# A graph network's edge sweep: node columns in the count windows in place of part columns and a placing matrix

## Chip, cores and metric

One core of a Trainium2 chip runs the whole kernel. The metric is the device time of one execution in microseconds; the kernel before took 1702.9 us (median of three runs, 1701.83 to 1708.91). The engines are called PE (matrix products; PEld is its weight load), VectorE (DVE in the rows), ScalarE (ACT), GpSimd (POOL) and SyncE (SP).

## What is computed

One graph convolution over 6,250 nodes of 256 features and 200,000 edges sorted by destination, a residual product, a top-2 mixture of 64 experts, a batch norm and a layer norm. What matters here is the sum over edges:

```python
deg_out = jnp.clip(jax.ops.segment_sum(ones, src, num_segments=n), 1.0)
deg_in = jnp.clip(jax.ops.segment_sum(ones, dst, num_segments=n), 1.0)
h = feats * jax.lax.rsqrt(deg_out)[:, None]
m = jax.ops.segment_sum(h[src], dst, num_segments=n) * jax.lax.rsqrt(deg_in)[:, None]
gc = m @ W_gc + b_gc
x = gc + (feats @ W_res + b_res)
```

The destinations are drawn as 6250 times a squared uniform number, so low node numbers have many edges and high ones few. The kernel moves the product with `W_gc` ahead of the sum.

## The kernel before

The stages follow each other: out-degrees and projections (to 176 us of the profile), the sweep over the edges, routing, experts, norms. The change lies in the sweep, in `gnn_moe_kernel` and in `_plan`, which lays the sweep out when the program is built.

The sorted edges form 1,563 groups of 128 (one edge per partition). The plan cuts them in two. The first groups, whose destinations lie close together, are *dense*: they are counted. The rest are *gathered*.

A dense chunk is a window of 128 columns. It has n parts, each of k groups whose destinations span at most w nodes; `DENSE` lists (first group, k, w, n). For each group PE multiplies (`count`, L665) a one-hot of the source's row within its tile (`lo`, made by `lo_of` on VectorE, eight groups a call, L250) with a one-hot of source tile and destination within the part (`hotk`, made by `hot_of`, L652), into a PSUM bank `pc` of 128 x 50 x w numbers: how many edges go from a source to a node. `hot_of` makes as many groups in one call as fit in `LANES // w`, made even; `KB` buffers hold the calls, four banks hold `pc`. After a part's last group ScalarE copies the bank into the chunk's `counts` (L676) at a column that it reads from `places` (a register load per eight parts, L673). Columns are nodes plus the part's number: each part has columns of its own, and a node that two parts share stands twice. Then `multiply` takes the 50 source tiles (L681, L682: the count tile is the weight, the rows `hrow`, in two pieces that add up to full precision, are the moving side) and sums them in one bank. ScalarE copies the sums (L692), and `spread`, at tile 9 of the next chunk, multiplies them by a placing matrix `to` (L698; made on VectorE at L685 from `spos`, which a count of parts per column, `held`, corrects), which adds the columns of one node, and adds the rows that the chunk in front has already summed for the same nodes (the carry-over, `overd`, L700). `sums_done` copies the result and SyncE writes it to `z_dram`.

The gathered groups go in windows of 128 nodes from the last node down: GpSimd fetches 128 rows of 2 KB by index (`fetch`, L580) into a ring of eight tiles, VectorE makes a one-hot for four groups a call (L846), PE adds them up (L585, L586), and a carry-over product (L867) joins the windows.

The order of the sweep is written out by hand: a list of steps with planned costs. Chunk c + 1 is counted while chunk c is multiplied, its parts spread over the tiles 1 to 42:

```python
for j in range(n):
    todo.setdefault(1 + j * 42 // n, []).extend(range(g0 + j * k, g0 + j * k + k))
```

and gathers are put in evenly over the planned time, from 76 us on (`LEAD`):

```python
while n < len(rows) and now > LEAD + n * every:
    gather(n)
    n += 1
```

`x_step` adds, in some of the chunks, the choice of experts for two tiles of finished nodes: ten VectorE calls (`x_make`, `x_top`), two calls on ScalarE, four transposes and eight small products. What it has not done by the end of the sweep is left to the routing stage.

Of the kernel before, what the change touches and what calls it, by code (L numbers as in the profile page):

```python
# [75 lines left out]
def _plan():  # L76
# [16 lines left out]
    def fits(g, k, w, n):  # L93
        return span(g + (n - 1) * k, k) <= w and spread(g, (n - 1) * k) + n + w <= WIN

    def cost(k, w, n):
        return max(12.6 + n * k * (0.021 + w * 0.0208), 5.0 + n * (0.2 + w * 0.03))

    dense, g, pe = [], 0, 0.0
    while 16.0 + 1.03 * (pe + (NGU - g) * 0.265) < (NGU - g) * 1.42:  # L100
        best = None
        for w in range(2, 11):
            for k in range(1, 12):
# [7 lines left out]
                c = cost(k, w, n) - 0.265 * n * k  # L111
# [23 lines left out]
LANES = 36  # L135
# [11 lines left out]
def gnn_moe_kernel(ctx, tc, x_in, src, dst, bases, nexts, firsts, parts, lasts, W_gc, b_gc, W_res, b_res, Wg, bg, w1, b1, w2, b2,  # L147
# [23 lines left out]
    def f32(ap):  # L171
        return ap.bitcast(F32)
# [43 lines left out]
    with tc.tile_pool(name="edges", bufs=1) as ep, ExitStack() as later:  # L216
# [7 lines left out]
        spos = ep.tile([128, ND], F32, name="spos")  # L224
# [38 lines left out]
        with tc.tile_pool(name="late", bufs=1) as lp, tc.tile_pool(name="both", bufs=2) as bp, \  # L263
# [6 lines left out]
            ones_b = dp.tile([128, 1], BF16, name="ones_b")  # L270
            V.memset(ones_b, 1.0)
# [45 lines left out]
            for c, (g0, k, w, n) in enumerate(DENSE):  # L317
                S.activation(rows_w[:, 2, c:c + 1], ones[:, c:c + 1], AF.Copy, scale=float(n - 1 + w))
            S.activation(rows_w[:, 1, :], rows_w[:, 0, :], AF.Copy, scale=-1.0, bias=float(WIN - 1))
            at_or_past = {}  # L320
# [3 lines left out]
            pidx1 = dp.tile([128, 1], F32, name="pidx1")  # L324
            G.tensor_scalar(pidx1, pidx, 1.0 - 64.0, None, op0=ALU.add)
            half_b = dp.tile([128, 1], BF16, name="half_b")
            G.memset(half_b, 0.5)
            npos = dp.tile([128, ND], F32, name="npos")
# [46 lines left out]
            def windows():  # L375
# [9 lines left out]
                G.tensor_tensor(spos, first[:, :ND], neg[:, :ND], ALU.add)  # L385
                V.scalar_tensor_tensor(pos, part[:, 0, :], pidx, first[:, :ND], op0=ALU.add, op1=ALU.subtract)
                G.tensor_scalar(npos, pos, -1.0, 0.5, op0=ALU.mult, op1=ALU.add)
                G.tensor_tensor(okc, okc, first[:, :ND], ALU.subtract)
                G.tensor_tensor(okc, okc, rows_w[:, 2, :], ALU.add)
                G.tensor_tensor(part[:, 1, :], part[:, 1, :], part[:, 0, :], ALU.subtract)  # L390

            def off_parts():
                V.tensor_tensor(away[:, 0, :], part[:, 1, :], rows_w[:, 0, :], ALU.is_gt)
                V.tensor_scalar(away[:, 1, :], part[:, 1, :], 0.0, None, op0=ALU.is_lt)
                V.tensor_add(away[:, 0, :], away[:, 0, :], away[:, 1, :])

            def off_windows():
                V.tensor_scalar(away[:, 1, :], okc, float(WIN), None, op0=ALU.is_gt)
# [7 lines left out]
            def placed():  # L406
# [7 lines left out]
                V.scalar_tensor_tensor(spos, spos, pidx1, held, op0=ALU.add, op1=ALU.subtract)  # L414


            CG, FIRST_IND = 32, 9
            degp = ps_deg.tile([128, 2 * NT], F32, name="degp")
            held = ps_deg.tile([128, ND], F32, name="held")
# [37 lines left out]
            assert FIRST_IND + ND < NGR // CG  # L457
# [9 lines left out]
            for i in range(NGR // CG):  # L467
# [22 lines left out]
                if i >= FIRST_IND:  # L490
                    c = i - FIRST_IND
                    if c < ND:
                        at_or_past[c] = dp.tile([128, 128], BF16, name="ind", bufs=2)
                        S.activation(at_or_past[c], iota_f, AF.Sign, bias=npos[:, c:c + 1])
                    if 1 <= c <= ND:
                        T.matmul(held[:, c - 1:c], at_or_past[c - 1], half_b, start=True, stop=True)
                    if c == ND:
                        placed()
# [47 lines left out]
            V.tensor_scalar(okc, okc, pidx, None, op0=ALU.is_gt)  # L546
# [13 lines left out]
        with tc.tile_pool(name="xs", bufs=1) as xs, tc.tile_pool(name="hotg", bufs=2) as hg, \  # L560
# [32 lines left out]
            def sums_done(pg, c):  # L593

                res = rsp.tile([WIN, D + 2], F32, name="resd" if c < ND else "resg")
                S.copy(res, pg)
# [3 lines left out]
                return res  # L600

            ends_met = {}

# [30 lines left out]
            KB = 2  # L634
            hots, los, live = {}, {}, {}

            def lo_of(q):

                if q * PAIRS < GD:
# [966 lines left out]
```

## Time and profile before

| | us |
|---|---|
| median of three runs | 1702.9 |
| the profiled execution | 1725.73 |
| its span, first to last instruction | 1723.7 |
| PE busy | 1485.0 (86%) |
| VectorE busy | 925.1 (54%) |
| ScalarE busy | 710.7 (41%) |
| GpSimd busy | 877.0 (51%) |

The time of the profiled execution is 2 us longer than its span; it is 1.3% above the median of the runs. A view gives start and length in us of an instruction (or of several like ones, x2), its engine, line, operation and tiles, and in brackets how long the engine stood idle before it and what ended that. PE's ends are modelled: starts are what tells its pace. The granted clock of PE is a share of its upper level, 2.4 GHz. The view by stretch gives for each stretch its length and the busy times of PE, PEld, DVE, ACT and POOL, each with its count of instructions, then the granted clock, the busy share of the DMA engines and what they moved in GB/s.

### The profile page before, as it was taken

Reading aid. Unit: us, or ns where it says so; the run is one execution under the profiler, and the core shown is the slowest. Engines: PE = TensorE matmul, PEld = TensorE weight load, DVE = VectorE, ACT = ScalarE, POOL = GpSimd, SP = SyncE. Lnnn points to the kernel's source line nnn. Section 1 sums busy time; section 2 is a strip of 40 time slices with the busy share of each in tenths; the row PEclk is TensorE's granted clock in tenths of the full one; section 3 lists DMA queues with packets and bytes.
Section 4 is the critical chain, followed back from the end, with each engine's and each line's share of the span. In section 5 each row is a group of like instructions: output and inputs, shape, how many; then the busy total and the mean of one; then the engine's idle time right before and its main releaser. Section 6 shows DMA issues by size and latency. Waiting matters only on the chain. (4 is left out here: it accounts for less than half of the span.)

```text
span 1723.7 us, 31285 instructions
## 1 busy us (share of the span) xinstructions
PE 1485.0 (86%) x10475; PEld 1246.4 (72%) x10475; DVE 925.1 (54%) x1790; ACT 710.7 (41%) x1740; POOL 877.0 (51%) x918
## 2 busy tenths in 40 slices
PE   6999587889999999999999986579999999999730
PEld 3555476778888889898988885368878877777620
DVE  9999865655564555554544545922222222221796
ACT  3443643434565555455554442222222222222248
POOL 6000137776776767667777752046655656554000
PEclk9999679999999999999999997689999999999875
DMA  6899766667767777777767764648868887775924
GB/s 183 255 275 264 221 192 173 184 187 212 202 199 195 203 205 205 207 203 209 204 197 202 207 181 116 165 145 259 244 206 253 268 251 241 205 244 168 240 78 131
DMA packets 217941, 352.50 MB, mean 205 GB/s; under 512 B 24214, under 2 KB 148886, under 8 KB 217770
## 3 DMA queue, kind: packets, MB, share of 16 engines
q1 hardware_dynamic: 158422, 180.22, 35.7%
q0 software_dynamic: 52448, 163.08, 33.3%
q10 hardware_dynamic: 6900, 7.10, 1.5%
q8 instruction: 86, 1.41, 0.3%
q14 instruction: 85, 0.70, 0.1%
HBM read 269.43 MB, written 74.47 MB: 200 GB/s over the span
## 5 line engine op out<-in xcount | busy, mean ns | idle before, releaser
L580 POOL DMA_INDIRECT r<-h_dram,srcg x502 | 558.3, 1112 | 285.9 <-issue 131.6
L681 PE MATMUL sm<-hrow,counts 125*128 125x258 f32 x1650 | 539.9, 344 | 7.6 <-ACT counts L676 7.4
L676 ACT CAST counts<-pc 128x300 f32 (+7 forms) x840 | 376.4, 448 | 323.4 <-PE pc L665 161.1
L682 PE MATMUL sm<-hrow,counts 125*128 125x256 f32 x1650 | 445.7, 286 | 1.6 <-issue 1.6
L681 PEld LDWEIGHTS sm<-hrow,counts 125*128 125x128 f32 x1650 | 328.0, 199 | 33.7 <-issue 18.8
L665 PE MATMUL pc<-hotk,lo 128*128 128x300 bf16 (+7 forms) x1061 | 298.6, 318 | 61.8 <-issue 35.1
L652 DVE TENSOR_TENSOR hotk<-key,iota_h 128x1800 bf16<-128x1800 f16 (+5 forms) x209 | 201.2, 963 | 248.6 <-PE pc L665 117.0
L682 PEld LDWEIGHTS sm<-hrow,counts 125*128 125x128 f32 x1650 | 322.6, 195 | 2.4 <-issue 1.2
L1360 ACT ACTIVATE hT<-ph,b1c 128x128 f32<-128x128 f32 (+8 forms) x256 | 108.3, 437 | 350.9 <-PE ph L1358 202.5
L1370 PE MATMUL py<-w2s,hT 128*128 128x256 f32 (+3 forms) x992 | 241.9, 386 | 7.8 <-ACT hT L1360 5.6
L1358 PE MATMUL ph<-xgT,w1s 128*128 128x128 f32 (+8 forms) x1024 | 210.7, 349 | 3.5 <-ACT hT L1360 2.2
L1370 PEld LDWEIGHTS py<-w2s,hT 128*128 128x128 f32 (+3 forms) x992 | 166.3, 176 | 50.0 <-issue 7.8
L1358 PEld LDWEIGHTS ph<-xgT,w1s 128*128 128x128 f32 x1024 | 170.4, 192 | 37.2 <-issue 15.3
L1324 POOL DMA_INDIRECT y_dram<-ys,dest x124 | 120.0, 968 | 139.8 <-DVE ys L1373 69.0
L1324 POOL DMA_INDIRECT xg<-x_dram,ids x124 | 120.1, 969 | 104.7 <-DVE ids L1275 65.4
L585 PE MATMUL pg<-r,hot 128*128 128x258 f32 x502 | 167.0, 333 | 6.2 <-DVE hot L846 2.5
L665 PEld LDWEIGHTS <-lo 128*128 128x128 bf16 x1061 | 95.6, 105 | 85.4 <-issue 23.6
L1373 DVE TENSOR_TENSOR ys<-py,b2s 128x256 f32<-128x256 f32 (+3 forms) x124 | 51.4, 420 | 175.8 <-PE py L1370 112.2
L586 PE MATMUL pg<-r,hot 128*128 128x256 f32 x502 | 142.7, 284 | 0.0
L1348 DVE COPY xgT<-pte 128x256 f32<-128x256 f32 (+7 forms) x64 | 38.5, 601 | 171.5 <-PE pte L1346 72.9
L846 DVE TENSOR_TENSOR hot<-keyg,iota_f 128x512 fp32r<-128x512 f16 (+3 forms) x135 | 87.7, 651 | 49.9 <-PE pc L665 20.6
L250 DVE TENSOR_TENSOR lo<-lo_b,iota 128x1024 bf16<-128x1024 bf16 x133 | 91.1, 686 | 43.2 <-PE pc L665 31.9
(325 smaller groups left out, 1755.4 us busy)
## 6 DMA issues: line engine op xcount, KB each, us to landing
w1s<-in_L_gnn_w_dram SPq DMA_DIRECT2D x64, 512.0 KB
w2s<-in_L_gnn_w_dram SPq DMA_DIRECT2D x64, 512.0 KB
y_dram<-zeros SPq DMA_DIRECT2D x48, 256.0 KB
yr<-y_dram SPq DMA_DIRECT2D x25, 448.0 KB
b2s<-in_L_gnn_b_dram SPq DMA_DIRECT2D x64, 128.0 KB
r<-h_dram,srcg POOLq DMA_INDIRECT x502
h_dram<-hrow SPq DMA_DIRECT2D x5, 1344.0 KB
z_dram<-zeros ACTq DMA_DIRECT2D x7, 903.0 KB
```

The costliest lines, as they stand in the source:

```text
L580: G.indirect_dma_start(out=f32(r[:, :2 * D]), out_offset=None, in_=h_dram[:, :], in_offset=bass.IndirectOffsetOnAxis(ap=idx, axis=0))
L585: T.matmul(pg, hot, r[:, D:], start=first, stop=False)
L586: T.matmul(pg[:, :D], hot, r[:, :D], start=False, stop=last)
L652: V.tensor_tensor(hot, pairs(key, e, n, m), iota_h[:, None, :m, :].to_broadcast([128, n // 2, m, 2]), ALU.is_equal)
L665: T.matmul(pc, los[g // PAIRS][:, r // 2, :, r % 2], hots.pop(g), start=(i == 0), stop=(i == k - 1))
L676: S.copy(counts[c % 2][:, :, ds(live["at"][j % 8], w)], pc.rearrange("p (t w) -> p t w", w=w))
L681: T.matmul(sm, by, hrow[:, t, D:], start=(t == 0), stop=False)
L682: T.matmul(sm[:, :D], by, hrow[:, t, :D], start=False, stop=(t == NT - 1))
L1324: w = G.indirect_dma_start(**kw)
L1358: T.matmul(ph[:, :m], w1s[:, kk, c * 128:(c + 1) * 128], xgT[:, kk, :m], start=(kk == 0), stop=(kk == 1))
L1360: S.activation(hT[:, c, :m], ph[:, :m], AF.Gelu, bias=b1_e[:, c:c + 1])
L1370: T.matmul(py[:n], hT[:, c, k * 128:k * 128 + n], w2s[:, c, :], start=(c == 0), stop=(c == 3))
```

## The change

The columns of a window are nodes. A part's first column is left out of ScalarE's copy, and VectorE adds it to the column that stands there (`carried`, L675), one part later in program order. With that the parts' numbers no longer take columns, a window holds more nodes, and the placing matrix, `held`, `spos` and the 33 Sign calls that fed them are gone. The plan prices VectorE too: 30 dense chunks, 1,118 counted groups in 909 parts (before 33, 1,061 and 840) and 445 gathered groups (502). The one-hots come in calls of half the size, four buffers for two: 488 calls with 335,800 columns (before 209 with 323,100). The carry-over enters the sums at tile 25 of its own chunk, ScalarE copies them once, and the last chunk gets the gathered rows by one more product (`last_rows`). The calls of `x_make` and `x_top` are handed out over several tiles; 23 pairs of tiles are done in the sweep (before 22). The window arrays on the host follow.

```diff
-        return span(g + (n - 1) * k, k) <= w and spread(g, (n - 1) * k) + n + w <= WIN
+        return span(g + (n - 1) * k, k) <= w and spread(g, (n - 1) * k) + 1.0 + w <= WIN
 
     def cost(k, w, n):
-        return max(12.6 + n * k * (0.021 + w * 0.0208), 5.0 + n * (0.2 + w * 0.03))
+        return max(12.6 + n * k * (0.021 + w * 0.0208), 5.0 + n * (0.2 + w * 0.03), 4.0 + n * (0.18 + k * (0.09 + w * 0.035)))
...
-    while 16.0 + 1.03 * (pe + (NGU - g) * 0.265) < (NGU - g) * 1.42:
+    while 16.0 + 1.03 * (pe + (NGU - g) * 0.265) < (NGU - g) * 1.68:
...
-LANES = 36
+LANES = 18
+
+APART = [c[1] * 128 * (N * max(_node(c[0]), 0.5)) ** 0.5 >= NE for c in DENSE]
...
-            KB = 2
-            hots, los, live = {}, {}, {}
+            KB = 4
+            hots, los = {}, {}
...
                 T.matmul(pc, los[g // PAIRS][:, r // 2, :, r % 2], hots.pop(g), start=(i == 0),
                          stop=(i == k - 1))
+                if i == k - 1:
+                    if j % 8 == 0:
+                        _, live["at"] = nc.values_load_multi_w_load_instructions(
+                            places[c:c + 1, j:j + 8], engines=(ACT_E, DVE_E), min_val=0, max_val=WIN - w,
+                            skip_runtime_bounds_check_because="clipped to what the window leaves")
+                    carried(1)
+                    at, pc = live["at"][j % 8], pc.rearrange("p (t w) -> p t w", w=w)
+                    if j == 0:
+                        live["adds"], live["carry"] = [], []
+                        live["puts"] = [S.copy(counts[c % 2][:, :, :w], pc).ins]
+                    else:
+                        put = S.copy(counts[c % 2][:, :, 1:][:, :, ds(at, w - 1)], pc[:, :, 1:])
+                        for a in live["adds"]:
+                            tc.declare_no_dep(put.ins, a, reason="other columns of the window")
+                        live["carry"].append((counts[c % 2][:, :, ds(at, 1)], pc[:, :, 0:1], APART[c]))
+                        live["puts"].append(put.ins)
                 if g % PAIRS == 1:
                     lo_of(g // PAIRS + 1)
                 if g == cuts[cut_of[g]][1] - 1:
                     hot_of(cut_of[g] + KB)
-                if i == k - 1:
-                    if j % 8 == 0:
-                        _, live["at"] = nc.values_load_multi_w_load_instructions(
-                            places[c:c + 1, j:j + 8], engines=(ACT_E,), min_val=0, max_val=WIN - w,
-                            skip_runtime_bounds_check_because="clipped to what the window leaves")
-                    S.copy(counts[c % 2][:, :, ds(live["at"][j % 8], w)], pc.rearrange("p (t w) -> p t w", w=w))
+                if i == k - 1 and j == n - 1:
+                    carried(0)
+
+            def carried(but):
+
+                while len(live["carry"]) > but:
+                    to, more, apart = live["carry"].pop(0)
+                    add = V.tensor_tensor(to, more, f32(to), ALU.add).ins
+                    j = len(live["adds"])
+                    tc.add_manual_dep(add, live["puts"][j + 1].name, SYNCED, reason="its bank, and the column of the part in front")
+                    for a in live["puts"][j + 2:]:
+                        tc.declare_no_dep(add, a, reason="columns behind it")
+                    for a in live["adds"][:None if live["between"] else -1] if apart else ():
+                        tc.declare_no_dep(add, a, reason="another column of the window")
+                    live["adds"].append(add)
+                    live["between"] = False
...
-                if t == 25:
-                    to = rsp.tile([128, WIN], F32, name="to")
-                    V.tensor_scalar(to, iota_f, spos[:, c:c + 1], okc[:, c:c + 1], op0=ALU.is_equal,
-                                    op1=ALU.mult)
-                    live["to"] = to
-                    if c:
-                        live["over"] = rows_of(c, "overd")
+                if c and t == 9:
+                    live["over"] = rows_of(c, "overd")
+                if c and t == 25:
+                    T.matmul(sm, live["over"], ends_met["dense"], start=False, stop=False)
                 if t == NT - 1:
-                    sums = rsp.tile([128, D + 2], F32, name="sums")
-                    S.copy(sums, sm)
-                    live["sums"] = sums
-
-            def spread(c):
-
-                pw = banks[c % 2][:, :D + 2]
-                T.matmul(pw, live["to"], live["sums"], start=True, stop=(c == 0))
-                if c:
-                    T.matmul(pw, live["over"], ends_met["dense"], start=False, stop=(c < ND - 1))
-                if c == ND - 1:
-                    T.matmul(pw, rows_of(ND, "overd"), ends_met["gather"], start=False, stop=True)
-                ends_met["dense"] = sums_done(pw, c)
+                    res = rsp.tile([WIN, D + 2], F32, name="resd")
+                    S.activation(res, sm, AF.Copy, scale=okc[:, c:c + 1])
+                    ends_met["dense"] = res
+                    if c < ND - 1:
+                        sums_done(res, c)
+
+            def last_rows():
+
+                pw, res = banks[(ND - 1) % 2][:, :D + 2], ends_met["dense"]
+                T.matmul(pw, rows_of(ND, "overd"), ends_met["gather"], start=True, stop=True)
+                V.tensor_tensor(res, pw, res, ALU.add)
+                sums_done(res, ND - 1)
...
                 def of_one_hots(c):
                     g0, k, w, n = DENSE[c]
-                    return n * k * (0.23 + 0.034 * w)
+                    return n * (0.18 + k * (0.09 + 0.035 * w)) + 4.0
```

What stands on VectorE between two counts, in the middle of the sweep. Before: one-hots for gathers, for the counts (`hotk`), for source rows (`lo`), and the two matrices `to` and `overd`.

```order
L250 TENSOR_TENSOR lo<-lo_b,iota_78 128x1024 [waits PE_49]
L846 TENSOR_TENSOR hot<-keyg,iota_f 128x512 [waits PE_49]
L652 TENSOR_TENSOR hotk<-key,iota_h 128x1800 [waits PE_49]
L685 TENSOR_SCALAR to<-iota_f,spos,okc 128x128
L590 TENSOR_SCALAR overd<-iota_f,shift 128x128
```

After (the same kind of place): the register step (ISA) and the add of a part's first column, which waits for ScalarE, stand between the one-hots, and the register load of the next eight places.

```order
L871 TENSOR_TENSOR hot<-keyg,iota_f 128x512
L571 TENSOR_SCALAR overg<-iota_f,shift 128x128
L675 ISA
L675 TENSOR_TENSOR counts_2888<-pc,counts_2888 128x50 [waits Activation_49]
L251 TENSOR_TENSOR lo<-lo_b,iota_78 128x1024
L633 TENSOR_TENSOR hotk<-key,iota_h 128x600 [waits PE_49]
L650 TENSOR_LOAD places
```

Calls on `hotk` went from 1800 to 600 columns, `to` went away, and in all 879 adds and 127 loads came.

On PE, where the sums of one chunk are placed while the next is multiplied. Before: the placing product and the carry-over, in a bank of the chunk in front, between two multiplies.

```order
L681 MATMUL sm_3066<-hrow,counts_3031 128x258
L682 MATMUL sm_3066<-hrow,counts_3031 128x256
L698 MATMUL sm_3065<-sums,to 128x258
L700 MATMUL sm_3065<-resd,overd 128x258
L585 MATMUL pg<-r_3056,hot 128x258
```

After: the carry-over alone (L693), in the bank in which the multiplies of its own chunk add up.

```order
L646 MATMUL pc<-hotk,lo 128x400
L688 MATMUL sm_2923<-hrow,counts_2888 128x258
L689 MATMUL sm_2923<-hrow,counts_2888 128x256
L693 MATMUL sm_2923<-resd,overd 128x258
L566 MATMUL pg<-r_2920,hot 128x258
```

The product with `to` and the copy of the sums behind which it waited are gone from PE's order.

## Rows read from the trace of the kernel before

**Rows 1.** Busy time of each engine by stretch: us, engines, granted clock, DMA

```profile
0.00:176.00 176.00, 157.78 (x1905) 91.69 (x1906) 166.46 (x154) 70.20 (x229) 31.37 (x96) 0.98 0.84 243
176.00:242.00 66.00, 42.84 (x264) 35.28 (x262) 54.22 (x108) 42.34 (x130) 11.81 (x27) 0.61 0.72 216
242.00:436.00 194.00, 166.45 (x1208) 147.91 (x1208) 107.67 (x179) 81.43 (x202) 138.66 (x123) 0.95 0.68 188
436.00:1024.00 588.00, 556.39 (x4178) 518.96 (x4177) 309.80 (x650) 308.94 (x691) 412.27 (x373) 0.99 0.72 203
```

**Rows 2.** Timeline of ScalarE, the copies that end chunks 0, 6 and 32

```profile
241.57 0.37 ACT L692 COPY sums<-sm 128x258 f32<-128x258 f32 x1 [2.38 <-issue]
...
437.59 0.38 ACT L692 COPY sums<-sm 128x258 f32<-128x258 f32 x1 [1.78 <-PE sm L682]
...
1045.47 0.38 ACT L692 COPY sums<-sm 128x258 f32<-128x258 f32 x1 [4.93 <-PE sm L682]
```

**Rows 3.** Timeline of PE, from one count to the next

```profile
402.62 0.48 PE L665 MATMUL pc<-hotk,lo 128*128 128x350 bf16 x2
402.82 0.41 PE L681 MATMUL sm<-hrow,counts 125*128 125x258 f32 x1
...
403.18 0.28 PE L585 MATMUL pg<-r,hot 128*128 128x258 f32 x1
403.30 0.28 PE L586 MATMUL pg<-r,hot 128*128 128x256 f32 x1
...
403.67 0.48 PE L665 MATMUL pc<-hotk,lo 128*128 128x350 bf16 x2
```

**Rows 4.** Timeline of PE, placing product and carry-over

```profile
488.52 0.60 PE L698 MATMUL sm<-sums,to 128*128 128x258 f32 x2
488.96 0.60 PE L700 MATMUL sm<-resd,overd 128*128 128x258 f32 x2
```

**Rows 5.** Costliest groups: line, operation, count | busy us, mean ns | idle before, releaser

```profile
L580 POOL DMA_INDIRECT r<-h_dram,srcg x502 | 558.3, 1112 | 285.9 <-issue 131.6
...
L676 ACT CAST counts<-pc 128x300 f32 (+7 forms) x840 | 376.4, 448 | 323.4 <-PE pc L665 161.1
...
L652 DVE TENSOR_TENSOR hotk<-key,iota_h 128x1800 bf16<-128x1800 f16 (+5 forms) x209 | 201.2, 963 | 248.6 <-PE pc L665 117.0
...
L846 DVE TENSOR_TENSOR hot<-keyg,iota_f 128x512 fp32r<-128x512 f16 (+3 forms) x135 | 87.7, 651 | 49.9 <-PE pc L665 20.6
L250 DVE TENSOR_TENSOR lo<-lo_b,iota 128x1024 bf16<-128x1024 bf16 x133 | 91.1, 686 | 43.2 <-PE pc L665 31.9
```

**Rows 6.** Timeline of VectorE: small calls, and calls near two gathers

```profile
173.34 0.21 DVE L535 TENSOR_SCALAR s_out<-pd 125x50 f32<-125x50 f32 x1 [0.37 <-PE pd L533]
173.47 0.20 DVE L538 TENSOR_REDUCE dmax<-pd 125x1 f32<-125x50 f32 x1
...
697.17 0.89 DVE L652 TENSOR_TENSOR hotk<-key,iota_h 128x1400 bf16<-128x1400 f16 x1 [4.94 <-PE pg L586]
...
706.42 0.17 DVE L720 RECIPROCAL s_in<-s_in 125x2 f32<-125x2 f32 x1 [2.92 <-issue]
706.62 0.89 DVE L722 SCALAR_TENSOR_TENSOR xr<-z,s_in,xr 125x256 f32<-125x256 f32 x2
```

**Rows 7.** Groups by form in the sweep (us 200 to 1046), count one-hots

```profile
L652 DVE TENSOR_TENSOR hotk<-key,iota_h 128x1800 bf16<-128x1800 f16 x62 | 67.8, 1095 | 88.2 <-PE pc L665 32.6 <-PE sm L682 25.4 <-PE pg L586 16.0
...
L652 DVE TENSOR_TENSOR hotk<-key,iota_h 128x900 bf16<-128x900 f16 x1 | 0.6, 629 | 1.3 <-PE pc L665 1.3
```

**Rows 8.** Line 673, ScalarE's queue: duration ns min, median, max; first and last start

```profile
L673 ACTq TENSOR_LOAD <-places x120: 539/560/2944, 177.4 to 1024.5; - x120
```

**Rows 9.** Timeline of GpSimd, two gathers

```profile
697.37 1.51 POOL L580 DMA_INDIRECT r<-h_dram,srcg  x1 [1.45 <-PE pg L586]
...
704.56 0.95 POOL L580 DMA_INDIRECT r<-h_dram,srcg  x1 [0.30 <-issue]
```

More of the change, by code (lines that the diff above doesn't have):

```diff
@@ L413, in placed @@
                 V.tensor_copy(places, pp[:, :NPM])
-                V.scalar_tensor_tensor(spos, spos, pidx1, held, op0=ALU.add, op1=ALU.subtract)
-            CG, FIRST_IND = 32, 9
+            CG = 32
             degp = ps_deg.tile([128, 2 * NT], F32, name="degp")
-            held = ps_deg.tile([128, ND], F32, name="held")
             def turned(t):
@@ L489, in gnn_moe_kernel @@
                     masks[i]()
[L490 to L498, printed above, removed]
+                if i == 12:
+                    placed()
                 turned(i + 1)
@@ L591, in rows_of, with sums_done @@
                 return to
-            def sums_done(pg, c):
-                res = rsp.tile([WIN, D + 2], F32, name="resd" if c < ND else "resg")
-                S.copy(res, pg)
+            def sums_done(res, c):
                 row = nc.values_load(base_i[0:1, c:c + 1], engines=(SP_E,), min_val=0, max_val=N,
@@ L599, in sums_done @@
                 nc.sync.dma_start(out=z_dram[ds(row, WIN), :], in_=res)
-                return res
             ends_met = {}
+            live = {"between": False, "carry": []}
             banks = [ps_s.tile([128, 512], F32, name=f"sm{i}") for i in range(2)]
@@ L646, in hot_of @@
                     return
+                live["between"] = True
                 a, b, w = cuts[q]
@@ L842, in hot_rows @@
                     return
+                live["between"] = True
                 i, g = rows[n]
@@ L867, in gather @@
                         T.matmul(live["pg"], live["overg"], ends_met["gather"], start=False, stop=True)
-                    ends_met["gather"] = sums_done(live["pg"], ND + i)
+                    res = rsp.tile([WIN, D + 2], F32, name="resg")
+                    S.copy(res, live["pg"])
+                    sums_done(res, ND + i)
+                    ends_met["gather"] = res
                     made["gathered"] = i
@@ L938, in gnn_moe_kernel @@
                     add_rows(pg, ring[0], hot, True, True)
-                    res = rsp.tile([WIN, D + 2], F32, name="res_e", tag="sums")
+                    res = rsp.tile([WIN, D + 2], F32, name="res_e", tag="resg")
                     S.copy(res, pg)
@@ L947, in gnn_moe_kernel @@
                 z, xr = x_load(rows_at(z_dram), rows_at(r_dram), 1)
[L948 removed]
+                for run in x_make(z, xr, 1, rows_at(x_dram)):
+                    run()
                 x_logits(banks[1], x_turn(banks[0], xr, 1), 1)
@@ L951, in gnn_moe_kernel @@
                 mosti = ge.tile([TP, 1, 2], U32, name="mosti")
-                x_top(banks[1], 1, most, mosti)
+                for run in x_top(banks[1], 1, most, mosti):
+                    run()
                 V.tensor_copy(top[:, ds(ti, 1), :], most)
```

89 lines of the change are left out of this document (45 added, 44 removed).

## The prediction

> **What bounds the kernel now.** I read the busy table by stretch first. Of a span of 1723.7 us the sweep, the part that the change rewrites, takes the 870 us from 176 to 1047; in the stage before it VectorE is busy 166 of 176 us [rows 1]. ScalarE's copy of the sums (L692) ends each chunk: chunk 0 at 241.6, chunk 6 at 437.6, chunk 32 at 1045.5 [rows 2]. So chunks 1 to 6 took 196.0 us and chunks 7 to 32 took 607.9, 803.9 in all. In the late stretch PE is busy 556 of 588 us, VectorE 310, ScalarE 309; in the early one PE 166 of 194, VectorE 108 [rows 1]. PE leads, but a modelled end hides short waits, so I price PE's work by distances between starts. From one count to the next of the same kind 1.05 us pass, with two counts of 350 columns and three pairs of f32r matmuls, a matmul every 0.118 [rows 3]. A pair (one multiply of a tile, or one gathered group) is thus 0.237 us. A count of 350 columns is (1.05 - 3 x 0.237) / 2 = 0.17 us; I split it into 0.417 ns a column, one a cycle at the upper level of 2.4 GHz, which is granted nearly throughout there [rows 1], and 0.021 us. Two f32 matmuls (L698) start 0.44 us before the next two (L700) [rows 4].
>
> PE's work in chunks 1 to 32 before: 1,600 multiplies 379; 907 counts with 292,550 columns 141; 502 gathers 119, their 29 carry-overs 13; placing and carry-over of sums 28; twelve small matmuls, taken at 0.11, for each of 22 expert choices 29. That is 710 us in 803.9: the chunks took 1.13 times PE's work, 1.10 in the late stretch (554 of 608), 1.25 in the early one (156 of 196). The early loss has its sign in the row of the one-hots: L652 was idle 249 us in all before its calls, 117 of it waiting for counts on PE [rows 5], since a buffer comes free only when its last group is counted, and there are two.
>
> **The change, part by part.** *PE.* The plan now has 30 chunks and 445 gathered groups for 33 and 502, 1,118 counted groups for 1,061. 150 multiplies fewer: 35.5 us. 57 gathers fewer: 13.5. 33 placing products (0.44 each): 14.5. Three carry-overs of sums and two of gathers: 2.2. Added: 57 counts and 15,500 columns, 7.7, and one more pair of expert choices, 1.3. PE loses 57 us of work.
>
> *VectorE's adds.* 879 calls on 50 elements, one operand from PSUM. No such call stands in the trace; nearest is L535, 50 elements from PSUM, 0.21 us, and the next independent call starts 0.13 after it. A call that waits for the one in front starts 0.03 behind its end: L722 follows a call of 0.17 at 0.20 [rows 6]. So an add holds VectorE for 0.13 to 0.24; by the new order 430 of the 879 wait for an earlier VectorE call, and I take 0.18.
>
> *One-hots in small calls.* 1800 columns take 1.095 us, 900 take 0.629 [rows 7]: 0.518 ns a column and 0.163 fixed, of which 0.08 lies beside the next call. 488 calls for 209: +22 us; 12,700 columns more: +7. Four buffers of half the size hold as much as two did and come back sooner; below zero this could give back part of the 117 us of waits, so its price lies between +29 and nothing.
>
> *Register loads.* VectorE now reads the parts' places itself, 127 loads. On ScalarE one takes 0.56 us [rows 8], partly beside the call in front: between 0 and 0.56, I take 0.25, 32 us. The register step ahead of each add is hidden by the call before it; without that cover it belongs to the add's upper bound.
>
> *Less on VectorE:* 33 placing matrices (9 us), 14 gather one-hot calls at 0.65 (9).
>
> *Who is the bound, by chunk.* While chunk c is multiplied, chunk c + 1 is counted. In chunks 1 to 10 of the new plan VectorE has 423 adds (76 us), 244 one-hot calls with 143,900 columns (94), 71 calls of L250 at 0.6 (43), 59 loads (15), 48 gather one-hots at 0.6 (29), 33 carry-over matrices (9) and six expert choices of about 3.2 us (ten calls, an estimate from their like in [rows 6]; 19): 285 us. PE has there 500 multiplies (118), 568 counts with 141,900 columns (71), 192 gathers (51 with carry-overs), carry-overs of sums (4) and the choices (8): 253. **VectorE is longer by 32.** In chunks 11 to 29 (444 parts, 426 adds, 228 one-hot calls with 178,000 columns, 253 gathers, 17 choices) the same count gives VectorE 344 and PE 404. Bound: 285 + 404 = 689 us. At VectorE's higher share the waits are not those of either old stretch; I take a factor of 1.11, just above the late 1.10, because smaller pieces help and a VectorE near 90% hurts; 1.06 and 1.16 are the ends (730 and 799 us), the upper one past the old mean. The granted clock, 0.95 in the early stretch [rows 1], I leave: PE's share of work there, 253 of some 316 us, is that of before. 689 x 1.11 = 764.8, against 803.9: **-39**.
>
> *Opening.* 32 parts and 106 groups instead of 77 and 154 up to the end of chunk 0, in a stretch of 66 us where VectorE is busy 54, PE 43, ScalarE 42 [rows 1]. PE loses 4 us, ScalarE 45 copies at less than their mean of 0.45 [rows 5]; VectorE's smaller one-hots pay for its 30 adds. Between 0 and -8, I take **-3**.
>
> *Ends.* One f32 product and one copy fewer behind the last multiply: **-1**. Four tiles instead of six are left to the routing stage: **-1**. The 33 Sign calls and small products of the first stage cost nothing now, hidden under VectorE's 166 of 176 us, and give nothing back.
>
> *New waits.* An add waits for ScalarE's copy of its own part; behind it on VectorE stand the one-hots, and PE's count waits for both, with the multiplies and gathers queued behind it. A bank of `pc` is now freed by the add, which is issued after the next part's copy; of four banks three parts remain as slack, 1.5 us at early density and 3 late. The add's copy is normally done by then. SP's window writes fall from 63 to 58 and come earlier; SP is not waited for.
>
> *The gathers' queue.* A gather call is 0.95 us while VectorE idles (704.56; VectorE idle 2.92 up to 706.42) and 1.51 beside a one-hot call (697.37) [rows 6, 9]; the mean is 1.112 [rows 5], with 0.30 between calls, 711 us for 502. With VectorE's share going from 53% (417 of 782 us, [rows 1]) to 82% (629 of 765) the stretch of 0.167 grows to 0.26, so a gather takes 1.21 and with the gap 1.51 us: 290 us in chunks 1 to 10, level with VectorE's 285, and 382 in the others, under PE's 404. If each VectorE call with two SBUF inputs held a gather up for its whole length, L652, L250 and L846 (380 us, [rows 5]) would have made each of the 502 gathers 0.95 + 0.76 + 0.30 = 2.0 us, 1,000 us in all, more than the whole sweep; so the rows show a hold-up, not the full one, and the sum stays. In full, the new kernel's 428 us of these calls over 445 gathers would make 2.2 us each (rival d). The Trainium skill, SBUF — State Buffer, section "SBUF: two separate sides", states this lock for the whole instruction; it speaks against a change that gives VectorE more calls, and the trace agrees only in part: 1.112 us on average where the lock in full would give 1.7.
>
> **Sum.** -39 - 3 - 1 - 1 = -44 us. The profiled execution took 1725.7 us; it would become 1681. The median of the runs shown is 1702.9, 1.3% below it, and its three runs lie within 0.4%; I take the difference as it is: **1658 us**.
>
> **Rivals.** (a) *PE stays the bound in every chunk.* With adds at 0.13 and loads hidden VectorE has 249 us in chunks 1 to 10, less than PE's 253. Then 253 + 404 = 657, times the old late 1.10 is 723: -81, and with opening and ends -5 it gives 1617. For it: half of L652's idle time was waiting for PE, so VectorE has room. Against: single early chunks still have more VectorE work than PE work, and all adds would have to be independent.
> (b) *VectorE bounds the whole sweep, slower.* Place: the add. If VectorE reaches it before ScalarE's copy is through (0.45 us, mean [rows 5]), it idles with its queue behind it. At 0.35 us an add the sets are 357 and 416, 773 times 1.11 is 858: +54 - 5 gives 1752. It decides from about 0.28 us an add, where 327 + 404 = 731, times 1.11 less 5, is the old time. Against it: ScalarE is busy half of the time [rows 1], and three parts of slack.
> (c) *No change.* Either adds near 0.27 (323 + 404, times 1.11 is 807: 1701), or the gathers' queue: every call at 1.51 makes 437 x 1.81 = 791 us from the first use of a gathered row (about 253) to 1044, plus 10 for the last row's way, 7 past the old end: 1710. For it: both engines come close to PE early.
> (d) *Gathers locked out by VectorE in full:* 437 x 2.2 = 961 us from 253, 1224 with the last row, +177: 1880. The rows speak against it, as said above. The rule behind it is the one of the Trainium skill, SBUF — State Buffer, named there.
> (e) *It does not do what it says:* the adds could be serialized by waits left in; the new order shows 430, which are priced.
>
> **How the numbers follow.** The forecast, 1630 to 1692, has 0.57; (a) 0.12; (c) 0.14; (b), with what (e) would add, 0.16; (d) 0.01. Half a per cent, 8.5 us, is what a measurement of this kernel can tell from no change. Faster: 0.57, 0.12 and 0.04 of (c), 0.73; same: the rest of (c), 0.10; slower: 0.17. The range leaves out (b), (d) and the lower part of (a): 1622 to 1706.
>
> **What would show it.** Adds (L675) near 0.2 us and 879 of them; VectorE's share above 90% in chunks 1 to 10 and 80 to 88% later; the copies at L696 about 31 us apart in chunks 1 to 10 and 23.6 later, chunk 0 ending near 239, chunk 29 near 1003; gathers at a mean near 1.2. It would be wrong if PE's counts waited for adds in the late chunks, if ScalarE's copies were what the adds wait for, or if the early chunks took over 340 us.

## The result, and the profile after

The changed kernel took 1643.7 us (median of four runs, 1641.0 to 1649.4), the kernel before beside it 1705.9 (1701.8 to 1711.4): a ratio of 0.964, 95% interval 0.960 to 0.968, or 62 us. Forecast were 44, with a range that holds the result. The profiled execution of after (1641.0) lies 2.7 us under its median, that of before (1725.7) 20 above, so the traces differ by 85, their spans by 84. Some 20 us of the difference between these two traces thus come from the profile of before and not from the change.

One thing has to be known for all that follows. The level went with the chip: in the first eight experiments, on one chip, the kernel before took 1640 and 1641 us, in the last four, on another, 1700, near the 1706 of the first comparison, whose chip is not on record. So times are compared as ratios to the kernel before that ran beside them, and traces at one level. The traces at the higher level also lack records: that of before in the first comparison has 18,167 semaphore events, that of the same program in experiment 1 30,284. How long an engine stood idle can be read there, what ended it less surely, and a wait for "issue", that is for nothing that the profile shows, can be one whose record is missing.

Busy time by stretch of the changed kernel, first comparison (us, PE, PEld, DVE, ACT, POOL, granted clock, DMA; the stretches end with chunk 0, chunk 10 and chunk 29):

```profile
174.00:226.50 52.50, 29.70 (x209) 25.04 (x209) 48.52 (x129) 27.35 (x82) 7.44 (x23) 0.67 0.82 249
226.50:552.10 325.60, 277.40 (x2070) 242.97 (x2069) 269.69 (x898) 167.66 (x468) 206.97 (x198) 0.99 0.68 186
552.10:972.40 420.30, 412.99 (x3122) 386.60 (x3121) 318.19 (x1044) 234.61 (x512) 262.75 (x247) 1.00 0.71 197
```

Against [rows 1, 2]: chunk 0 ends at 226.5 instead of 241.6 (-15); the chunks behind it take 745.9 us instead of 803.9 (-58); from the last copy to the end of the span 666.9 are left instead of 678.2 (-11). In the late stretch PE is busy 98% (before 95%), VectorE 76%; in the early one VectorE 83%.

The groups of the same trace that answer to [rows 5] (busy us, mean ns | idle before, releaser):

```profile
L561 POOL DMA_INDIRECT r<-h_dram,srcg x445 | 469.7, 1056 | 303.0 <-PE pc L646 86.6 <-PE sm L689 66.3 <-DMA z_dram<-resd 50.8
...
L633 DVE TENSOR_TENSOR hotk<-key,iota_h 128x800 bf16<-128x800 f16 (+4 forms) x488 | 250.8, 514 | 93.7 <-PE pc L646 58.9 <-PE sm L689 18.1 <-PE pg L567 6.9
L675 DVE TENSOR_TENSOR counts<-pc,counts 128x50 f32 x879 | 212.3, 241 | 50.6 <-issue 10.2 <-ACT counts L659 7.8 <-DVE counts L675 4.0
```

An add takes 0.241 us. The idle time before the one-hots fell from 249 us to 94, and a gather takes 1.056 us, not the 1.21 forecast.

### The profile page after: what moved, and what is told of

It is laid out like the page before. It is cut to its first block, busy times and chain, and to the rows that moved or that the text cites. A ratio compares the mean times of both kernels' runs of the same rounds, so it can differ in the third digit from the quotient of the medians.

```text
span 1639.3 us, 32636 instructions
## 1 busy us (share of the span) xinstructions
PE 1408.6 (86%) x10005; PEld 1171.4 (71%) x10005; DVE 1088.3 (66%) x2905; ACT 692.1 (42%) x1704; POOL 797.1 (49%) x859
## 5 line engine op out<-in xcount | busy, mean ns | idle before, releaser
L561 POOL DMA_INDIRECT r<-h_dram,srcg x445 | 469.7, 1056 | 303.0 <-PE pc L646 86.6
L688 PE MATMUL sm<-hrow,counts 125*128 125x258 f32 x1500 | 496.1, 345 | 3.9 <-DVE counts L675 3.7
L659 ACT CAST counts<-pc 128x200 f32 (+7 forms) x879 | 361.1, 411 | 262.1 <-PE pc L646 158.7
L689 PE MATMUL sm<-hrow,counts 125*128 125x256 f32 x1500 | 402.1, 282 | 0.0
L646 PE MATMUL pc<-hotk,lo 128*128 128x250 bf16 (+7 forms) x1118 | 307.7, 306 | 74.1 <-DVE counts L675 37.1
L688 PEld LDWEIGHTS sm<-hrow,counts 125*128 125x128 f32 x1500 | 292.4, 195 | 34.1 <-issue 24.1
L633 DVE TENSOR_TENSOR hotk<-key,iota_h 128x800 bf16<-128x800 f16 (+4 forms) x488 | 250.8, 514 | 93.7 <-PE pc L646 58.9
L689 PEld LDWEIGHTS sm<-hrow,counts 125*128 125x128 f32 x1500 | 287.8, 192 | 1.7
L675 DVE TENSOR_TENSOR counts<-pc,counts 128x50 f32 x879 | 212.3, 241 | 50.6 <-issue 10.2
L566 PE MATMUL pg<-r,hot 128*128 128x258 f32 x445 | 148.8, 334 | 0.5 <-issue 0.5
L423 PE MATMUL pr<-wcat,fT 128*125 128x512 f32 x200 | 101.3, 631 | 3.5 <-DMA wcat<-in_L_gnn_W_res_dram 3.5
```

The source lines that it names most:

```text
L561: G.indirect_dma_start(out=f32(r[:, :2 * D]), out_offset=None, in_=h_dram[:, :], in_offset=bass.IndirectOffsetOnAxis(ap=idx, axis=0))
L566: T.matmul(pg, hot, r[:, D:], start=first, stop=False)
L633: V.tensor_tensor(hot, pairs(key, e, n, m), iota_h[:, None, :m, :].to_broadcast([128, n // 2, m, 2]), ALU.is_equal)
L646: T.matmul(pc, los[g // PAIRS][:, r // 2, :, r % 2], hots.pop(g), start=(i == 0), stop=(i == k - 1))
L659: put = S.copy(counts[c % 2][:, :, 1:][:, :, ds(at, w - 1)], pc[:, :, 1:])
L675: add = V.tensor_tensor(to, more, f32(to), ALU.add).ins
```

## The experiments

**1. The kernel before again.** No edit.

> The kernel before, once more, for a second trace. The profiled execution of before took 1725.7 us, 20 us above the median of its runs (1705.9). If the 20 us lie in the sweep, a nearer trace has the copy that ends chunk 32 near 1026 instead of 1045.5 and the change gave about 53 us there; if they lie in the stage before or behind the sweep, the copy stays near 1040 and the sweep's gain is 65 to 73 us, more than the medians differ.

1642.0 us; nowhere near the 1703 to 1726 of the first comparison, so neither of the two cases came true. Its stretches to the end of chunk 0, over chunks 1 to 6, and over chunks 11 to 32:

```profile
174.00:240.60 66.60, 40.27 (x260) 33.30 (x258) 54.01 (x108) 41.97 (x129) 12.42 (x27) 0.67 0.70 213
240.60:413.10 172.50, 162.21 (x1226) 142.42 (x1224) 109.72 (x181) 82.97 (x204) 135.31 (x123) 1.00 0.74 209
...
503.00:973.80 470.80, 470.14 (x3617) 445.04 (x3615) 256.31 (x538) 257.90 (x554) 334.51 (x314) 1.00 0.74 214
```

Chunks 1 to 32 in the first trace, then in this one, and the one-hots' row of this one:

```profile
241.60:1045.50 803.90, 744.63 (x5559) 688.13 (x5557) 420.69 (x842) 394.16 (x902) 554.94 (x500) 0.98 0.70 196
```

```profile
240.60:973.80 733.20, 722.25 (x5560) 671.15 (x5558) 423.64 (x842) 399.64 (x902) 538.93 (x499) 1.00 0.75 215
...
L652 DVE TENSOR_TENSOR hotk<-key,iota_h 128x1800 bf16<-128x1800 f16 (+5 forms) x209 | 201.8, 967 | 204.7 <-PE pc L665 203.6
```

On this chip PE is busy 470.1 of 470.8 us late. Chunks 1 to 32 take 733.2 us for 710 of PE's work, where the first trace had 803.9. PE's instructions are the same. Of the 71 us that are gone 48 are time in which PE stood (59 in the first trace, 11 here), and 22 lie in PE's busy time, with a granted clock of 0.98 there and 1.00 here. The one-hots still stand 204 us waiting for counts: with PE busy nearly throughout, that row is no sign of a loss.

**2. Small one-hot calls alone**, in the kernel before (two scratch tiles of the repair path share a buffer to make room).

```diff
-LANES = 36
+LANES = 18
-            KB = 2
+            KB = 4
```

> The kernel before with the one-hots of the counts in calls of half the size and four buffers. Theory 1 (the gain is the 57 us of work taken from PE; the small calls only cost VectorE time that lies under PE): no change, 1700 to 1715. Theory 2 (the small calls let PE wait less: before, PE lost some 41 us in waits between 450 and 1000 and 32 us to a lowered clock between 200 and 1050; after, 18 and 2): 25 to 50 us faster, 1655 to 1680.

1633.8 against 1640.0 us, ratio 0.996 (0.994 to 0.998). A gain of 6 us: near the "no change" of theory 1, far from the 25 to 50 of theory 2. But both were made for a level of 1706, and here PE hardly waited before (experiment 1); what small calls give at the higher level was not tried.

**3. Big one-hot calls** in the changed kernel: the first edit backwards (`LANES` 36, `KB` 2), so that size of the calls and number of buffers change together.

> The changed kernel with the one-hots in calls of the old size, two buffers. Theory 1: as the changed kernel, 1634 to 1654, since VectorE has 25 us of calls less and PE's work is the same. Theory 2: the waits come back, 25 to 50 us slower than the changed kernel, 1669 to 1694, with PE's busy share in chunks 11 to 29 falling from 98% to about 93%.

1619.0 us, ratio 0.987 (0.984 to 0.989); the changed kernel has 0.979 on the same chip (experiment 5). So the small calls give 0.8%, 13 us; neither theory had that (none, or 25 to 50). Line 675, adds, what VectorE waited for before them and how long PE's counts waited for them, first with big calls, then with small ones (experiment 5); the last two numbers are us and times:

```profile
L675 DVE TENSOR_TENSOR counts<-pc,counts x879: 213/244/265, 185.0 to 940.2; 128x50 f32 x176
...
  ACT counts L659: 45.2, 72
...
  PE pc L646: 44.6, 78
```

```profile
L675 DVE TENSOR_TENSOR counts<-pc,counts x879: 214/242/335, 187.4 to 925.5; 128x50 f32 x176
...
  ACT counts L659: 12.1, 33
...
  PE pc L646: 35.5, 70
```

With big calls VectorE stands 45 us at adds whose copy on ScalarE is not through, with small ones 12, and PE's counts wait 45 and 36 us for adds. That calls of half the size fill the time up to the copy would fit this; it is argued, not shown. The chunks behind chunk 0, with big calls:

```profile
228.50:539.10 310.60, 273.49 (x2068) 240.82 (x2066) 262.92 (x743) 168.39 (x469) 215.24 (x199) 0.99 0.68 195
539.10:958.40 419.30, 413.87 (x3124) 386.83 (x3122) 312.56 (x937) 234.77 (x513) 267.52 (x247) 1.00 0.70 197
```

They take 729.9 us together, 3 less than the 733.2 of the kernel before (experiment 1).

**4. Without the adds.** The adds and their register steps are left out; the body of `carried` only empties its list:

```diff
-                    add = V.tensor_tensor(to, more, f32(to), ALU.add).ins
...
-                    live["adds"].append(add)
```

> The changed kernel without the 879 adds of a part's first column (their register steps go too); these columns are left out of the sums. Theory 1 as predicted (VectorE bounds chunks 1 to 10 by 32 us of work): 423 adds of 0.24 us are 102 us less on VectorE there, PE becomes the bound at 253 us, 30 to 40 us less in these chunks, nothing in the later ones: 1604 to 1614. Rival (PE's work and its chain of waits set the pace in all chunks, adds lie beside it): 0 to 10 us faster, 1634 to 1644. Rival (adds held up PE's counts and so the late chunks too, 50 us of waits for adds in the trace): 45 us or more, under 1600.

What follows the sweep computes with other sums and runs other loops (12,519.7 us in all), so only the sweep is read, in one trace against one. It ends at 915.4 instead of 943.5 (experiment 5), 28 us sooner; 16.5 of them lie in chunks 1 to 10 (282.9 for 299.4), 7 in the late chunks, 5 in the opening. So 212 us of adds cost 28, 0.03 us each. None of the cases came true: the early chunks gain less than the 30 to 40 of theory 1, the sweep more than the 0 to 10 of the first rival and less than the 45 of the second. What is late next shows in who PE waited for in chunks 1 to 10, first without the adds, then with them (us in total, times, longest):

```profile
PE pg L566 <- DMA r<-h_dram,srcg: 14.5, 22, 1.7
```

```profile
PE pc L646 <- DVE counts L675: 24.4, 54, 1.0
PE pg L566 <- DMA r<-h_dram,srcg: 1.0, 2, 0.6
```

With the adds gone PE waits for gathered rows instead.

**5. The changed kernel again.** No edit.

> The changed kernel itself, beside the kernel before, since the kernel before took 1640 us in the first four experiments and 1706 in the first comparison; there PE was busy 94% of chunks 7 to 32, in the second trace of before 99 to 100%. Theory 1 (what the change gives is what PE still waited for before, plus PE's work of 57 us less what VectorE costs in the early chunks): where before runs at 1640 the change gives 10 to 25 us, 1615 to 1630. Rival (the 62 us of the first comparison are the work itself and hold wherever it runs): 1575 to 1585. Rival (small calls cost VectorE time that shows wherever PE has no other waits; the big calls gave 1619): 1630 to 1642, no change against before.

1605.0 against 1641.1 us, ratio 0.979 (0.977 to 0.981), 36 us: more than the 10 to 25 expected, far less than the work's 57, and the last rival (no change) fell. Stretches of this run:

```profile
174.00:228.70 54.70, 30.80 (x209) 26.25 (x209) 49.70 (x133) 28.55 (x85) 8.37 (x23) 0.66 0.80 242
228.70:528.10 299.40, 271.73 (x2066) 239.31 (x2064) 265.77 (x898) 167.83 (x469) 210.74 (x198) 1.00 0.71 202
528.10:943.50 415.40, 411.79 (x3124) 386.27 (x3124) 318.56 (x1046) 235.03 (x512) 254.12 (x248) 1.00 0.71 199
```

Against experiment 1: chunk 0 ends 12 us sooner, the chunks behind it take 714.8 instead of 733.2 (-18), the rest 660.2 instead of 666.1 (-6): together the 36. By the prediction's prices PE's work in the chunks fell by 53 us (710 to 657), and what they take beyond it grew from 23 to 58, of which 46 lie in chunks 1 to 10 (299.4 for 253): there VectorE is busy 89%. Without the small calls (experiment 3) the chunks would have gained 3 us, not 18.

**6. Two dense chunks fewer**, 40 groups more gathered.

```diff
-    while 16.0 + 1.03 * (pe + (NGU - g) * 0.265) < (NGU - g) * 1.68:
+    while 16.0 + 1.03 * (pe + (NGU - g) * 0.265) < (NGU - g) * 1.48:
```

> The changed kernel with two dense chunks fewer: 28, with 40 groups more gathered (485). PE: two chunks of 16.8 us off, 40 gathers of 0.265 on, 23 us less. Theory 1 (PE sets the pace in the late chunks, GpSimd has slack: a gather takes 1.06 us and 0.30 between two, 485 of them 660 us of a sweep of some 700): 10 to 23 us faster than the changed kernel. Rival (the gathers' queue becomes the bound, or the gathers' one-hots, 10 calls of 0.65, and the same work in fewer chunks only lengthen VectorE's early chunks): no change or up to 10 us slower.

1597.3 us, ratio 0.976 (0.972 to 0.980) against 0.979 (0.977 to 0.981) of the changed kernel: 8 us by the medians, between the two cases, and the intervals overlap (five of the six runs lie between 1592.8 and 1600.5, one at 1614.5). PE's 23 us came back by a third. In chunks 1 to 10 PE now waits for gathered rows, where it had waited 1.0 us (experiment 4):

```profile
PE pg L566 <- DMA r<-h_dram,srcg: 13.7, 18, 1.6
```

**7. Two chunks fewer and big calls** (the edits of 3 and 6).

> The changed kernel with 28 chunks and with the one-hots in calls of the old size, two buffers. If both parts act by themselves, it stands to the 28 chunks as the big calls stand to the changed kernel, and should be the fastest so far: 1596 to 1610 where the big calls took 1619. Rival (gathers' queue bounds at 28 chunks): as the big calls, 1615 to 1630.

1606.4 us, ratio 0.980 (0.978 to 0.982): 0.7%, some 12 us, under the big calls with 30 chunks, as the first case had it, but 9 over experiment 6, not "the fastest so far", which reckoned without the small calls' worth.

**8. The first chunk as before**: 20 parts of 2 groups.

```diff
-                c = (cost(k, w, n) if g else 4.0 + n * (0.18 + k * (0.09 + w * 0.035))) - 0.265 * n * k
+                c = cost(k, w, n) - 0.265 * n * k
```

> The changed kernel with the first chunk cut as before: 20 parts of 2 groups for 10 parts of 4; all other chunks as they are. The opening (stage start to the end of chunk 0) came out 13 to 15 us shorter than before where 3 were forecast. If ten parts fewer are the cause: 8 to 12 us slower than the changed kernel. Rival (the cause lies in chunk 1, which is counted while chunk 0 is multiplied: 22 parts and 66 groups for 57 and 114): 0 to 4 us slower.

1612.9 us, ratio 0.984 (0.981 to 0.987), 8 us slower than the changed kernel. That is at the lower end of the first case. In the traces chunk 0 ends at 233.5 instead of 228.7, 5 us later (the profiled execution, 1608.4, is the fastest of its four). So ten parts fewer account for some 5 of the 12 us; the rest, chunk 1's smaller count beside chunk 0's multiplies, was not tried alone.

**9 to 12. On the chip where before takes 1700 us.** The choices of experts late:

```diff
-                twice = c >= ND - 2
+                twice = c >= ND - 7
...
-                    if c and (c, t) != (ND - 1, 38):
+                    if c >= 10 and (c, t) != (ND - 1, 38):
```

> The changed kernel with the choices of experts for two tiles taken out of chunks 1 to 10: they begin in chunk 11 and come twice in each of the last seven chunks instead of the last two; 23 pairs as before. If VectorE bounds chunks 1 to 10 (they took 299 us in the second trace of the changed kernel, for 253 us of PE's work): six pairs of some 3.2 us on VectorE, 19 us, leave the early chunks, 8 us of PE's work come into the late ones, which PE bounds: 8 to 15 us faster than the changed kernel (1605). Rival (the early chunks wait for the chain of count, copy and add, which no other work on VectorE lengthens): early chunks as they were, late ones 6 to 10 us longer, 1610 to 1615.

1655.2 us, ratio 0.973 (0.970 to 0.976); the changed kernel did not run beside it; it had 0.964 (0.960 to 0.968) in the first comparison, and experiment 10, close to it, 0.965, so this is slower. Chunks 1 to 10 took 318.3 us, 7 less than in the first trace of the changed kernel, the late ones 442.0, 22 more, of which chunks 23 to 27 have 21, with 24 to 29 us each where they had 21 to 22. The early part went the way the theory had it, with 7 us for 19 taken from VectorE; the late price was mis-sized.

A part priced at 0.24 us in the plan (30 chunks), and the same with 28:

```diff
-        return max(12.6 + n * k * (0.021 + w * 0.0208), 5.0 + n * (0.2 + w * 0.03), 4.0 + n * (0.18 + k * (0.09 + w * 0.035)))
+        return max(12.6 + n * k * (0.021 + w * 0.0208), 5.0 + n * (0.2 + w * 0.03), 4.0 + n * (0.24 + k * (0.09 + w * 0.035)))
...
-    while 16.0 + 1.03 * (pe + (NGU - g) * 0.265) < (NGU - g) * 1.68:
+    while 16.0 + 1.03 * (pe + (NGU - g) * 0.265) < (NGU - g) * 1.76:
```

(1.58 instead of 1.76 for 28 chunks; the first chunk's price likewise.)

> The changed kernel, its plan made with a part priced at 0.24 us on VectorE instead of 0.18 (0.24 is what an add took in the traces): still 30 chunks and 444 gathered groups, but 816 parts for 909, with wider parts of two groups in chunks 5, 6, 7 and 9. VectorE loses 93 adds and 12 register loads, some 29 us, and gets 28,000 columns of one-hots more, 15 us; PE gets 12 us of columns. If VectorE bounds the early chunks: 5 to 14 us faster than the changed kernel, 1591 to 1600. Rival (PE's work counts there too, or the adds lie beside it): 0 to 12 us slower, 1605 to 1617.

> The same price of a part with two chunks fewer: 28 chunks, 484 gathered groups, 776 parts. If both gains add up: 8 us (the measured gain of 28 chunks) under the kernel with the higher price, 1583 to 1592. Rival (with 484 gathers GpSimd, whose calls follow each other at 1.25 us at best, is the next bound): as the 28 chunks alone, 1594 to 1600.

30 chunks: 1641.7 us, ratio 0.965 (0.962 to 0.968), no difference from the changed kernel's 0.964, between the two cases: 93 adds fewer about paid for 12 us of columns on PE. 28 chunks: 1677.8, ratio 0.986 (0.983 to 0.990), **36 us slower** than with 30, by the kind of step that gave 8 us on the other chip (experiment 6); neither case had that. Chunks 1 to 10 and the rest, and what PE waited for over both stretches, with 30 and with 28 chunks:

```profile
230.20:550.20 320.00, 281.18 (x2070) 246.93 (x2068) 263.08 (x815) 146.27 (x376) 215.25 (x199) 0.99 0.66 189
550.20:969.30 419.10, 412.08 (x3119) 385.77 (x3117) 320.40 (x1047) 234.02 (x512) 255.80 (x246) 1.00 0.69 197
...
PE pc L646 <- DVE counts L675: 17.8, 35, 1.0
PE pc L646 <- issue: 16.0, 28, 1.5
```

```profile
229.20:590.30 361.10, 303.86 (x2154) 267.37 (x2152) 274.36 (x839) 147.59 (x379) 246.14 (x230) 0.95 0.67 192
590.30:1002.10 411.80, 385.82 (x2875) 358.36 (x2874) 295.51 (x968) 210.91 (x467) 271.71 (x255) 1.00 0.71 203
...
PE pc L646 <- issue: 36.6, 40, 3.1
PE pc L646 <- DVE counts L675: 22.8, 41, 3.1
...
PE pg L566 <- issue: 1.0, 2, 0.8
```

The early chunks, whose parts are the same, take 41 us more, with some 30 of the 40 added gathers among them and a granted clock of 0.95 for 0.99; late PE's share falls from 98% to 94%. PE's waits have grown before counts, by adds or by nothing that the trace names; before gathered rows it stands 1 us.

> All three: parts priced at 0.24, 28 chunks, and the choices of experts only from chunk 11 on (22 pairs find finished rows in time, one fewer, so six tiles are left to the routing stage instead of four, about 1 us). If VectorE bounds the early chunks and nothing else comes in its place: 1570 to 1585, the fastest of all. Rival (gathers bound at 28 chunks): 1590 to 1600.

1688.3 us, ratio 0.993 (0.990 to 0.995): 10 us over experiment 11, the late choices' loss once more. On the chip of experiments 1 to 8, 28 chunks came out 8 us faster than the changed kernel; no version was faster at both levels.

## Why the prediction was right, and where not

**The work on PE (-57) was right as a term, but did not make the gain alone.** Where PE hardly waited before (experiment 1), the late chunks run at 1.03 times PE's work after the change (415.4 for 404), and the sweep's end moved by the work less the new early waits. Of the 36 us there 18 lie in the chunks, and with big calls these would have gained 3 (experiment 3): the early waits eat nearly all that PE lost, which the prediction's 285 us on VectorE against 253 on PE said in kind. No run took work from PE and left the rest.

**The factor of 1.11 was the mis-sized term.** It stood for both stretches. Measured in the first comparison: chunks 11 to 29 420.3 us, 1.04 times PE's 404 (forecast 449), chunks 1 to 10 325.6, 1.14 times VectorE's 285 (forecast 316). Together 745.9 for 764.8, 19 us better. The old late loss of 1.10 was taken to stay; experiment 1 shows that it isn't a property of the pieces: on its chip the kernel before has 1.01 late. Why it vanished with the change at the higher level stays open. The 57 gathered groups fewer are one candidate: the sum priced them at PE's 0.237 us, 13.5 in all, and 40 more cost 36 us at that level (experiments 10 and 11). The small calls are another: they gave 13 us where PE had waited little. Neither was tried alone on a kernel at that level, so this part of the gain, some 26 us of the 62, is not shown. That the range held is in part luck: the sum took no difference of level into account, and on the other chip the change gave 36 us, with the small calls, the opening and the loss factor each off by 9 us or more.

**Who bounds, by chunk,** was right in kind. PE waited for adds in chunks 1 to 10 (24.4 us) and hardly later (3.1 from 528 to 943 in experiment 5), and experiments 4 and 9 shorten the early chunks by taking VectorE's work away (16.5 and 7 us). VectorE's excess was forecast at 32 us; taking 102 us of adds away gave 16.5 there, since gathered rows are late next. VectorE's share was 83% and 89%, not above 90%, and 76 to 77% late, not 80 to 88%. Rival (a), PE as the bound in every chunk, thus fell for the early chunks and describes the late ones.

**Adds.** Taken at 0.18 us, within 0.13 to 0.24; the record shows 0.241, at the upper end, and a register step of 0.069 ahead of each. Rival (b), slower from 0.28 on, was near by its price alone, but its mechanism did not come: VectorE waited 7.8 us for ScalarE's copies in the first trace of the changed kernel and 12.1 in the second, and the adds lie mostly under other waits, 0.03 us each. Nor did (e): an add waited 4.0 us in all for the one in front.

**Small calls** had been priced at +29 to nothing and taken at the upper end, through VectorE's sum. They gave 13 us (experiment 3): the sign was wrong. The row from which the other end was read, 117 us of one-hots waiting for counts [rows 5], could not have told: where PE hardly waits it shows 204 us, and small calls alone gave 6 there (experiments 1 and 2).

**Opening**: -3 forecast, -15 and -12 measured. It was priced by PE's work, but PE and ScalarE are busy about half of that stretch (31 and 29 of 55 us in experiment 5), and VectorE, busy 50 of it, lost only 4 us against experiment 1. How often the chain of one-hot, count and copy is gone through, 45 times less often now, may be what counts there. Experiment 8 shows 5 us for ten parts; for the rest this is argued only. Behind the sweep -2 were forecast, -11 measured in the first comparison and -6 between experiments 1 and 5; why was not looked into.

**Gathers** at 1.21 us were wrong: 1.056 and 1.045, against 1.112 and 1.082 before, though VectorE's share rose. The line through two calls [rows 6, 9] did not hold. The Trainium skill, SBUF — State Buffer, section "SBUF: two separate sides", limits its lock to certain VectorE operations, among them those with two SBUF inputs, and these only against a GpSimd operation that reads SBUF; the adds have one input in PSUM. The trace agrees with that part: 879 calls more, and the gather is 0.04 to 0.06 us shorter. It does not single the adds out, since the number of gathers and the one-hots changed too. Rival (d), the full lock, 2.2 us a gather, fell.

**Rival (c)**, the gathers' queue as the bound, fell for the changed kernel: PE waited 1.0 us for gathered rows in experiment 5. With 28 chunks it begins to show on the same chip (13.7 us, experiment 6). The 36 us of experiment 11 are something else: PE stood there before counts, not before gathered rows.

## What to carry to other kernels

Do not carry a stage's loss factor over to its successor: ask what the loss consists of, and price the waits that a change takes away as a term of their own. An engine with short jobs between those that others wait for can be better fed in small calls, even if its busy time for them grows by a fifth (one-hots 209 us in big calls, 251 in small). Idle time before a call is no loss as long as the engine that bounds the stage does not wait. A plan's balance between two engines that was tuned on one chip should keep some way from the edge: 40 more gathers gave some 8 us on one and cost 36 on another.

## What was not expected of the hardware

The same program took 1640 us on one chip and 1700 on another, with instructions of the same length (a gather 0.94 us at least on both, a one-hot call 0.963 and 0.967 on average) and a granted clock near 1 in the late chunks of both. On the slower chip the engines at times go on late. The timeline of experiment 11:

```profile
648.35 0.28 PE L567 MATMUL pg<-r,hot 128*128 128x256 f32 x1
648.46 0.10 PEld L646 LDWEIGHTS <-lo 128*128 128x128 bf16 x1
649.24 0.52 DVE L633 TENSOR_TENSOR hotk<-key,iota_h 128x700 bf16<-128x700 f16 x1 [1.37 <-PE pg L567]
649.29 1.38 ACT L659 CAST counts<-pc 128x300 f32 x3 [0.71 <-PE pg L567]
649.53 1.05 POOL L561 DMA_INDIRECT r<-h_dram,srcg  x1 [0.84 <-PE pg L567]
...
650.47 0.23 DVE L675 TENSOR_TENSOR counts<-pc,counts 128x50 f32 x1
...
650.76 0.32 PE L646 MATMUL pc<-hotk,lo 128*128 128x350 bf16 x1 [2.14 <-issue]
```

VectorE, ScalarE and GpSimd start again within 0.3 us of each other, 0.9 us and more behind the start of the matmul that is named as their releaser. PE follows 1.2 us later, after 2.14 us that the profile ascribes to nothing, but just behind the end of an add (650.47 and 0.23 us): this may be an ordinary wait whose record is missing. Counted over the chunks, the time in which PE, VectorE, ScalarE and GpSimd all stand still is 14.7 us in the first trace of before, 10.5 in experiment 11 and 2.4 in the first trace of the changed kernel, against 1.4 and 0.6 in experiments 1 and 5; so common stops are a part of what the higher level costs, not all of it. On the other chip PE's list of waits from 442 to 950 us of the kernel before is empty. What causes the late starts, and why more gathers bring more of them, stays open.

A register load of eight places takes 0.61 us in VectorE's queue (127 of them), near the 0.56 of ScalarE's [rows 8]. It isn't counted as busy, so VectorE may be fuller in the early chunks than its 89%; how much of a load lies beside other calls was not measured.
